# A two-layer graph-attention kernel: four-strip scores, smaller projection pieces, and a new order of work at the seams between batch entries

## The chip, the cores and the metric

The kernel runs on one core of one Trainium2 chip. The metric is the device time of one execution in microseconds (us); lower is better. Before the change three runs took 4387.88, 4392.93 and 4394.0 us, so the median is 4392.93 us. A separate profiled execution took 4391.85 us; its recorded span is 4389.8 us, and all durations below come from it.

Engines are called by the profile's names: PE is TensorE (PEld its weight loads), DVE is VectorE, ACT is ScalarE, POOL is GpSimd, SP is SyncE, which issues most of the DMAs.

## The reference

Input x has 8 batch entries of 2048 rows and 256 columns; adj is one 2048 x 2048 matrix of 0 and 1 for all entries. Two layers follow each other, each with a residual and a layer norm:

```python
# layer 0, for each entry: 8 heads of 32 columns
x_proj = einsum('bnd,hdf->bhnf', x, W)
e_src, e_dst = x_proj . a_src, x_proj . a_dst          # one number per row and head
e = leaky_relu(e_src[..., :, None] + e_dst[..., None, :], 0.2)
e = e + softplus(beta_tilde) * log(adj + 1e-6);  e = where(adj > 0, e, -huge)
h = softmax(e) @ x_proj;  x = layernorm(x + h.reshape(B, N, 256) @ W_out.T)
# layer 1, for each entry: one head of 256 columns
h1, h2, h3 = x @ W1, x @ W2, x @ W3
e = where(adj > 0, leaky_relu(h1 @ h2.T, 0.2), -huge)
x = layernorm(x + relu(softmax(e) @ h3))
```

All is in float32.

## The kernel before

**Layer 0 of an entry** is 64 steps (`Gat.step`, L320): 4 pairs of heads (`hp`) times 16 tiles of 128 source rows (`jt`). The exponential of the leaky score is split into factors of the two rows, so that a step needs no exponential: DVE makes, for each head of the pair, one 128 x 2048 tile `s` with one instruction (L336) from a row of factors `c` that is the same on all partitions, a column of factors `re` and the tile `mt` of the transposed mask. PE then adds `s` into the sums `val` (8 products) and mostly also into the denominators `den` (8 products), both in PSUM, in four strips of 32 output rows (`products`, L358). For some `jt`, listed in `SUMMED`, the `den` products are left out and DVE adds `s` into a tile `d` instead (L343; the first of them on ACT, L349). Four buffers hold `s`, two for each step, so DVE can be two steps ahead of PE. At the end of a head pair `finish` (L365) copies the sums to `ht` on ACT, takes the denominators through DRAM (`rc`, `rec_d`, `rb`) and, at every second pair, multiplies `ht` by their reciprocals on DVE (L389).

**The seam** leads an entry from layer 0 to layer 1. `output` (L391) yields four times; each time PE multiplies four row tiles of `ht` by W_out (products `y`, two row tiles in one PSUM buffer), DVE adds x and takes the statistics (L416 to L419), ACT normalises into `ht` (L425) and stores it. `turn` (L430) yields eight times; each time PE transposes two row tiles (`tr`, L439), ACT copies them to `x1t` (L440), and PE makes two row tiles of h3 (L445).

**Layer 1 of an entry** is 16 row tiles (`Dot`, L451). `scores` (L469) makes the 2048 scores `e` of a row tile on PE, adds the mask `pen` on DVE and takes the exponential on ACT into `p`, one row tile ahead; `Dot.step` (L484) transposes `p` (`pt`), and sums `acc` with h3.

**Interleaving.** The order of the PE instructions is the order of the program text; the framework orders the other engines. Layer 1 of entry b-1 is mixed with the layer 0 steps of entry b: `fill(0)`, `fill(1)` and `fill(2)` are the places in a `Dot.step` where steps (`layer_0`) or W_out products (`output`) are put. The last two row tiles of the entry before that are held back for the seam (L605, L606). All 64 steps of an entry are so spread over one period.

**Entry 0** has no layer 1 beside it. Its 64 steps are mixed with the projections of the other seven entries (`others`, L539): after every second step one group of four row tiles (`rows`, L255) with the eight transposes of x made one group ahead (`turn` in L549). There are 28 groups for 32 places. At an entry's last group `factors` (L268) and four `scale` (L282) run on DVE, and `store` (L288) sends v and re to DRAM; `queries` (L292) makes `c_d`. The entries come in the order 2, 3, 4, 5, 6, 7, 1; their `v` tiles take the two buffers "v" and "h3" in turn. Entry 1 stays in its buffer.

**The start.** `scores_first` (L246) makes the scores of entry 0 with the transposed x as the held operand and 16 moving columns: 32 products of 128 x 16.

PSUM has three buffers of 128 x 512 (`mm_tile`) that projections, transposes, y, e, tr and h3p share in turn. `chunk` has three buffers "ht" for `xg`, `xt`, `dn`, `h1` and adjacency rows.

## Time and profile before

| what | us |
|---|---|
| median of three runs | 4392.93 |
| span of the profiled execution | 4389.8 |
| PE idle, 0 to 100 | 23.5 |
| PE idle, 450 to 550 | 21.6 |
| PE idle, 1500 to 1600 | 6.8 |
| PE idle, 4000 to 4100 | 4.5 |
| granted PE clock, mean | 0.989 |

The table's idle times are the length of a stretch less PE's busy time in it. The page of a profile gives each engine's busy share, the share in 40 slices, the chain of work that ended last, and groups of instructions with count, busy time and mean duration. The order of time lists merged groups of one engine: start, length, engine, line, operation, output and inputs, and in brackets the idle time before it and what ended it. A matmul in float32 has two records. The lists of waits give total, number and longest.

### The profile page before, as it was taken

How to read it: one execution, taken by the hardware profiler on the slowest of the kernel's cores; microseconds unless marked ns; L12 is line 12 of the kernel's file. 1: busy time of each engine (PE TensorE's matmuls, PEld its weight loads, DVE VectorE, ACT ScalarE, POOL GpSimd, SP SyncE). 2: the span in 40 equal slices, each digit the busy share in tenths (PEclk: the TensorE clock that was granted, in tenths of full speed). 3: DMA queues.
4: the chain of work that ended last, by engine and by line, in shares of the span. 5: the costliest groups of instructions: out<-in, count | busy, mean ns of one | idle time of the engine just before them, and what ended most of it. 6: DMA issues, size and time to landing. Idle time of an engine off the chain costs nothing.

```text
span 4389.8 us, 59761 instructions
## 1 busy us (share of the span) xinstructions
PE 4243.0 (97%) x25052; PEld 2226.0 (51%) x25052; DVE 3624.5 (83%) x2597; ACT 1666.5 (38%) x3020; POOL 6.4 (0%) x14
## 2 busy tenths in 40 slices
PE   7899899999999999999999999999999999999999
PEld 5454344445444545445445454445555454545666
DVE  6888888998989898997989988898889889898222
ACT  6622233333333323333333334333333333333454
POOL 0000000000000000000000000000000000000000
PEclk9999999999999999999999999999999999999999
DMA  7887666656555554556555555556545565554111
GB/s 234 292 302 273 209 221 211 230 193 225 191 189 189 197 197 168 195 192 213 180 193 185 188 196 185 192 187 216 184 166 199 184 214 184 191 183 147 60 50 41
DMA packets 250958, 839.10 MB, mean 191 GB/s; under 512 B 32320, under 2 KB 150848, under 8 KB 175424
## 3 DMA queue, kind: packets, MB, share of 16 engines
q1 hardware_dynamic: 215360, 801.71, 52.1%
q10 hardware_dynamic: 35328, 33.56, 2.2%
q8 instruction: 196, 3.21, 0.3%
q14 instruction: 74, 0.61, 0.0%
HBM read 761.53 MB, written 73.14 MB: 190 GB/s over the span
## 4 chain that ended last, share of the span: by engine, by line
PE 56%; DVE 18%; issue 9%; DMA 4%; ACT 2%; SPq 1%; ACTq 0%; DVEq 0%
PE acc L510 15%; PE e L475 14%; DVE s L336 11%; PE val L361 11%; PE den L361 7%; DVE d L343 4%; PE pt L494 4%; DMA mt<-mt_d 3%; PE y L414 2%; PE h1p L465 2%; PE h3p L445 1%; DVE p L480 1%; ACT p L481 1%; DMA rc<-dn 1%; SPq L379 0%
## 5 line engine op out<-in xcount | busy, mean ns | idle before, releaser
L336 DVE SCALAR_TENSOR_TENSOR s<-c,re,mt 128x2048 f32<-128x2048 f32 x1024 | 2353.5, 2342 | 194.4 <-PE den L361 132.8
L361 PE MATMUL val<-s,v 128*32 128x512 f32 x8192 | 1030.0, 604 | 67.8 <-DVE s L336 67.3
L510 PE MATMUL acc<-h,pts 128*128 128x256 f32 x4096 | 949.9, 380 | 2.2 <-ACT pts L496 1.4
L475 PE MATMUL e<-x1t,h 128*128 128x512 f32 x2048 | 906.0, 595 | 6.8 <-ACT h L467 6.8
L510 PEld LDWEIGHTS acc<-h,pts 128*128 128x128 f32 x4096 | 748.1, 190 | 92.8 <-ACT pts L496 6.9
L361 PE MATMUL den<-s,re 128*32 128x512 f32 x5568 | 709.0, 599 | 3.3 <-ACT dn L376 3.3
L343 DVE SCALAR_TENSOR_TENSOR d<-s,re,d 128x2048 f32<-128x2048 f32 x272 | 632.2, 2344 | 0.0
L475 PEld LDWEIGHTS e<-x1t,h 128*128 128x128 f32 x2048 | 379.1, 190 | 459.5 <-issue 416.5
L496 ACT COPY pts<-pt 128x512 f32<-128x512 f32 x512 | 298.2, 583 | 766.4 <-PE pt L494 759.5
L361 PEld LDWEIGHTS val<-s,v 128*32 128x32 f32 x8192 | 244.3, 110 | 676.4 <-issue 516.3
L477 ACT ACTIVATE p<-e 128x512 f32<-128x512 f32 x512 | 303.1, 596 | 433.6 <-PE e L475 429.9
L480 DVE CUSTOM_DVE_ANT_0 p<-p,pen 128x2048 f32<-128x2048 f32 x128 | 292.9, 2288 | 198.2 <-ACT p L477 197.5
L361 PEld LDWEIGHTS den<-s,re 128*32 128x32 f32 x5568 | 194.3, 111 | 429.6 <-issue 417.0
L494 PEld LDWEIGHTS pt<-ident,p 128*128 128x128 f32 x2048 | 239.0, 141 | 223.2 <-issue 163.0
L481 ACT ACTIVATE p<-p,neg 128x2048 f32<-128x2048 f32 x128 | 256.7, 2006 | 242.4 <-DVE neg L480 242.4
L494 PE MATMUL pt<-ident,p 128*128 128x128 f32 x2048 | 319.3, 279 | 6.5 <-ACT p L481 6.5
L517 ACT ACTIVATE z<-acc,rec 128x256 f32<-128x256 f32 x128 | 60.9, 475 | 370.4 <-PE acc L510 340.0
L518 DVE TENSOR_TENSOR z<-z,x1r 128x256 f32<-128x256 f32 x128 | 53.8, 421 | 156.1 <-ACT z L517 155.9
L445 PE MATMUL h3p<-w3s,x1t 128*128 128x256 f32 x512 | 122.6, 383 | 15.4 <-ACT x1t L440 14.5
L414 PE MATMUL y<-wot,ht 128*128 128x256 f32 x512 | 120.5, 393 | 9.8 <-DVE ht L389 9.8
L262 PE MATMUL proj<-wp,xt 128*128 128x272 f32 (+1 forms) x512 | 125.5, 398 | 0.1
L349 ACT ACTIVATE d<-s,re 128x2048 f32<-128x2048 f32 x56 | 112.1, 2005 | 29.1 <-DMA mt<-mt_d 23.5
(85 smaller groups left out, 1877.3 us busy)
## 6 DMA issues: line engine op xcount, KB each, us to landing
mt<-mt_d SPq DMA_DIRECT2D x496, 1024.0 KB, 4.9
c<-c_d SPq DMA_DIRECT2D x64, 1024.0 KB, 7.1
pen<-pen_d SPq DMA_DIRECT2D x112, 512.0 KB, 3.4
xg<-in_x_dram SPq DMA_DIRECT2D x60, 512.0 KB, 6.0
adj_t<-in_adj_dram SPq DMA_DIRECT2D x16, 1024.0 KB, 7.9
mt_d<-mt SPq DMA_DIRECT2D x16, 1024.0 KB, 5.7
rb<-rec_d SPq DMA_DIRECT2D x64, 256.0 KB, 4.6
x_d<-ht ACTq DMA_DIRECT2D x32, 512.0 KB, 3.6
```

Of the source, the lines that this page charges most:

```text
L336: nc.vector.scalar_tensor_tensor(sa, self.cs[a], self.re[:, 0, jt, h:h + 1], mt, ALU.max, ALU.mult)
L343: nc.vector.scalar_tensor_tensor(d, sa, e[:, jt - 1, h:h + 1], d, ALU.mult, ALU.add)
L361: nc.tensor.matmul(dst[ts(q, DH), ts(c, BK)], weights[q % 2], s[q % 2][:, ds(q // 2 * HALF + c * BK, BK)], start=start, stop=stop)
L414: nc.tensor.matmul(y[:, i, :], self.ht[:, g * IG + k + i, kc, :], wot[:, kc, :], start=(kc == 0), stop=(kc == KC - 1))
L445: nc.tensor.matmul(t[:, ts(i, D)], x1t[:, kc, ts(2 * (j - 1) + i, P)], w3s[:, kc, :], start=(kc == 0), stop=(kc == KC - 1))
L475: nc.tensor.matmul(t, self.h1[:, kc, ts(it % IG, P)], self.x1t[:, kc, ts(c, BK)], start=(kc == 0), stop=(kc == KC - 1))
L477: nc.scalar.activation(p[:, ts(c, BK)], t, AF.Prelu, alpha=ALPHA)
L480: nc.vector.tensor_tensor_reduce(p, p, pen, -1.0, FMAX, ALU.add, ALU.min, neg)
L481: nc.scalar.activation(p, p, AF.Exp, bias=neg, scale=-1.0, accum_out=den)
L494: nc.tensor.transpose(t[:, ts(k, P)], p[:, ts(g * IG + k, P)], ident)
L496: nc.scalar.copy(pt, t)
L510: nc.tensor.matmul(acc, now[:, ts(k, P)], self.h3[:, j, :], start=(j == 0), stop=(j == NT - 1))
```

## The change

1. `scores_first` holds the weight columns (padded with zeros to 32, so `wp` is 16 columns wider) and moves the transposed x, in four strips: 8 products of 32 x 512. The result is copied to SBUF, transposed back by four transposes, and copied into `both`.
2. `others` yields after each row tile instead of each group of four (`rows` becomes `row`). The loop over entry 0's steps takes, after every second step, so many row tiles that the 112 are spread evenly over the 32 places: 3 and 4 in turn. The weights' preparation comes at each second step past 16 until it is done.
3. The entries come in the order 2, 3, 4, 5, 1, 6, 7. The buffers are still taken in turn, but entry 7, the last, takes "h3", as entry 6 does, since entry 1 stays in "v". `re` has three buffers.
4. Seams: the second held row tile has no W_out products in it; behind it come two times "two groups of W_out products, two steps". In `turn` two steps follow every second yield up to the sixth instead of one after each. At entry 0's seam four steps, the products in two halves and two steps.
5. `output` loads x two groups ahead.

```diff
+            t = mm_tile("scores")
+            for kc in range(KC):
+                for q in range(NB):
+                    nc.tensor.matmul(t[ts(q, DH), :], wp[:, kc, D:], xt[:, kc, ts(q, BK)],
                                      start=(kc == 0), stop=(kc == KC - 1))
+            s = chunk.tile([P, BK], F32, tag="pt", name="scores", bufs=2)
+            nc.scalar.copy(s, t)
+            t = mm_tile("scores_t")
+            for k in range(IG):
+                nc.tensor.transpose(t[:, ts(k, P)], s[:, ts(k, P)], ident)
...
-        items = [(gat, g) for gat in gats[2:] + gats[1:2] for g in range(NB)]
+        order = gats[2:-2] + gats[1:2] + gats[-2:]
...
-                gat.begin(("v", "h3")[n // NB % 2])
+                gat.begin("h3" if n // NB % 2 or gat is order[-1] else "v")
...
-        if k % 2 == 1:
-            next(pieces[0], None)
-            if k > NT and k % 4 == 1:
-                next(pieces[1], None)
+        if k % 2 == 0:
+            for _ in range(k * count // (NP * NT) - (k - 2) * count // (NP * NT)):
+                next(projections)
+            if k > NT:
+                next(weights, None)
...
-            layer_0(3)
-            output(4)
-            layer_0(1)
+            layer_0(4)
+            output(2)
+            next(projections)
+            output(2)
+            layer_0(2)
         else:
             dot.step(lambda k: layer_0((0, 0, 2)[k]))
-            dot.step(lambda k: (output((1, 1, 2)[k]), layer_0((0, 1, 1)[k])))
-        for _ in gat.turn():
-            layer_0(1)
+            dot.step()
+            for _ in range(2):
+                output(2)
+                layer_0(2)
+        for k, _ in enumerate(gat.turn()):
+            if k % 2 == 1 and k < 7:
+                layer_0(2)
         dot = Dot(gat)
-        dot.step(lambda k: layer_0((2, 1, 1)[k]))
+        dot.step(lambda k: layer_0((2, 0, 2)[k]))
```

More of the change, by code (lines that the diff above doesn't have):

```diff
@@ L105 @@
     beta_c = beta[:, 3:4]
-    wp = const.tile([P, KC, D + 2 * H], F32)
+    wp = const.tile([P, KC, D + DH], F32)
+    nc.vector.memset(wp[:, :, D + 2 * H:], 0.0)
     for kc in range(KC):
@@ L113 @@
         )
-    for a, dst in ((a_dst, wp[:, :, D:D + H]), (a_src, wp[:, :, D + H:])):
+    for a, dst in ((a_dst, wp[:, :, D:D + H]), (a_src, wp[:, :, D + H:D + 2 * H])):
         a_bc = small.tile([P, D], F32, tag="row", name="a_bc", bufs=4)
@@ L246, in scores_first, with row @@
         def scores_first(self, xt):
-            t = mm_tile("both")
-            for it in range(NT):
-                for kc in range(KC):
-                    nc.tensor.matmul(t[:, ts(it, 2 * H)], xt[:, kc, ts(it, P)], wp[:, kc, D:],
+            t = mm_tile("scores")
+            for kc in range(KC):
+                for q in range(NB):
+                    nc.tensor.matmul(t[ts(q, DH), :], wp[:, kc, D:], xt[:, kc, ts(q, BK)],
                                      start=(kc == 0), stop=(kc == KC - 1))
-            nc.scalar.copy(self.both.rearrange("p t h -> p (t h)"), t[:, 0:NT * 2 * H])
-        def rows(self, g, xt, scores=True):
-            cols = D + 2 * H if scores else D
-            for k in range(IG):
-                it = g * IG + k
-                t = mm_tile("proj")
-                for kc in range(KC):
-                    nc.tensor.matmul(t[:, 0:cols], xt[:, kc, ts(k, P)], wp[:, kc, 0:cols],
-                                     start=(kc == 0), stop=(kc == KC - 1))
-                nc.scalar.copy(self.v[:, it, :], t[:, 0:D])
-                if scores:
-                    nc.scalar.copy(self.both[:, it, :], t[:, D:cols])
+            s = chunk.tile([P, BK], F32, tag="pt", name="scores", bufs=2)
[3 more added lines that the diff above has]
+                nc.tensor.transpose(t[:, ts(k, P)], s[:, ts(k, P)], ident)
+            nc.scalar.copy(self.both.rearrange("p (q k) h -> p k q h", k=IG),
+                           t.rearrange("p (k q h) -> p k q h", k=IG, h=DH)[:, :, :, 0:2 * H])
+        def row(self, it, xt, scores=True):
+            cols = D + 2 * H if scores else D
+            t = mm_tile("proj")
+            for kc in range(KC):
+                nc.tensor.matmul(t[:, 0:cols], xt[:, kc, ts(it % IG, P)], wp[:, kc, 0:cols],
+                                 start=(kc == 0), stop=(kc == KC - 1))
+            nc.scalar.copy(self.v[:, it, :], t[:, 0:D])
+            if scores:
+                nc.scalar.copy(self.both[:, it, :], t[:, D:cols])
         def factors(self):
@@ L277, in factors @@
             nc.vector.tensor_tensor(ed, ed, top[:, 1:2, :].to_broadcast([P, NT, H]), ALU.subtract)
-            self.re = small.tile([P, 2, NT, H], F32, name="re", bufs=2)
+            self.re = small.tile([P, 2, NT, H], F32, name="re", bufs=3)
             nc.scalar.activation(self.re[:, 0], ed, AF.Exp, scale=-(1.0 - ALPHA))
@@ L302, in load @@
             nc.sync.dma_start(self.v, v_d[self.b])
-            self.re = small.tile([P, 2, NT, H], F32, name="re", bufs=2)
+            self.re = small.tile([P, 2, NT, H], F32, name="re", bufs=3)
             nc.sync.dma_start(self.re, re_d[self.b])
@@ L400, in load @@
                 nc.sync.dma_start(xs[g], xb[:, ts(g, IG), :])
-            for g in range(NB - 1):
-                load(g)
+            load(0)
+            load(1)
             for g in range(NB):
-                if g == 1:
-                    load(NB - 1)
+                if g + 2 < NB:
+                    load(g + 2)
                 st = small.tile([P, IG, nc.vector.BN_STATS_DIM], F32, name="st4", bufs=1)
@@ L531 @@
     for g in range(NB):
-        g0.rows(g, xt0[:, :, ts(g, BK)], False)
+        for k in range(IG):
+            g0.row(g * IG + k, xt0[:, :, ts(g, BK)], False)
         g0.scale(g)
@@ L539, in others @@
     def others():
-        items = [(gat, g) for gat in gats[2:] + gats[1:2] for g in range(NB)]
+        order = gats[2:-2] + gats[1:2] + gats[-2:]
+        groups = [(gat, g) for gat in order for g in range(NB)]
         xgs, xts = [], []
         def load(n):
-            if n < len(items):
-                xgs.append(load_x(items[n][0].b, items[n][1]))
+            if n < len(groups):
+                xgs.append(load_x(groups[n][0].b, groups[n][1]))
         def turn(n):
-            if n < len(items):
+            if n < len(groups):
                 xts.append(chunk.tile([P, KC, BK], F32, tag="ht", name="xt", bufs=3))
@@ L556, in others @@
         turn(0)
-        for n, (gat, g) in enumerate(items):
+        for n, (gat, g) in enumerate(groups):
             turn(n + 1)
             if g == 0:
-                gat.begin(("v", "h3")[n // NB % 2])
-            gat.rows(g, xts[n])
-            if g == 0 and n > 0:
-                items[n - 1][0].queries()
-            if g == NB - 1:
-                gat.factors()
-                for k in range(NB):
-                    gat.scale(k)
-                if gat.b > 1:
-                    gat.store()
-            yield
-        gats[1].queries()
+                gat.begin("h3" if n // NB % 2 or gat is order[-1] else "v")
+            for k in range(IG):
+                gat.row(g * IG + k, xts[n])
+                if g == NB - 1 and k == IG - 1:
+                    gat.factors()
+                    for i in range(NB):
+                        gat.scale(i)
+                    if gat.b > 1:
+                        gat.store()
+                if g == 0 and k == IG - 1 and n > 0:
+                    groups[n - 1][0].queries()
+                yield
+        order[-1].queries()
         yield
-    pieces = [others(), later_weights()]
-    for k in range(NP * NT):
+    projections, weights = others(), later_weights()
+    count = (B - 1) * NT
+    for k in range(1, NP * NT + 1):
         g0.step()
-        if k % 2 == 1:
-            next(pieces[0], None)
-            if k > NT and k % 4 == 1:
-                next(pieces[1], None)
+        if k % 2 == 0:
[3 more added lines that the diff above has]
+                next(weights, None)
     dot = None
```

## The prediction

> **What bounds the kernel now.** First the page's busy shares, then the waits of TensorE, then the order of time at three places.

> ```profile
> PE 4243.0 (97%) x25052; PEld 2226.0 (51%) x25052; DVE 3624.5 (83%) x2597; ACT 1666.5 (38%) x3020; POOL 6.4 (0%) x14
> ...
> PE val L361 <- DVE s L336: 67.3, 46, 5.7
> PE h3p L445 <- ACT x1t L440: 14.5, 8, 2.7
> ...
> PE y L414 <- DVE ht L389: 9.8, 2, 6.3
> ```

> PE is busy 97%, so at most 147 us can be won without removing products; 67.3 of them wait for the VectorE tiles `s`. The idle times come in three places. The start (0 to 160 us) holds 32 us of them. The steps 57 to 64 of entry 0 and its seam, from the order of time:

> ```profile
> 458.64 1.04 PE L361 MATMUL val<-s,v 128*32 128x512 f32 x2 [3.61 <-DVE s L336]
> 460.90 2.78 PE L361 MATMUL val<-s,v 128*32 128x512 f32 x11 [1.22 <-DVE s L336]
> ...
> 516.73 3.78 PE L414 MATMUL y<-wot,ht 128*128 128x256 f32 x8 [6.29 <-DVE ht L389]
> ```

> Here no projection is left, a step costs VectorE 2 x 2.27 = 4.53 us and PE 3.6, so PE waits at each step. And the later seams, the same to 0.1 us in each period of 509 us:

> ```profile
> 1536.16 1.04 PE L361 MATMUL val<-s,v 128*32 128x512 f32 x2 [1.53 <-DVE s L336]
> 1539.80 2.78 PE L361 MATMUL val<-s,v 128*32 128x512 f32 x11 [2.60 <-DVE s L336]
> ...
> 1567.01 1.99 PE L445 MATMUL h3p<-w3s,x1t 128*128 128x256 f32 x8 [2.70 <-ACT x1t L440]
> ...
> 1602.19 1.04 PE L361 MATMUL val<-s,v 128*32 128x512 f32 x2 [0.84 <-DVE s L336]
> 1604.45 1.49 PE L361 MATMUL val<-s,v 128*32 128x512 f32 x11 [1.22 <-DVE s L336]
> ```

> That is 8.9 us of idle a seam. Eleven records of `val` take 2.78 us at 1539.80 and 1.49 at 1604.45: the first ran at half clock, which costs 2.7 us more. VectorE itself stands idle there 1523.4 to 1529.05 (5.60, for y), 1554.2 to 1556.3 (2.11) and 1567.9 to 1572.6 (4.54).

> [...]

> **The change, part by part.**

> Scores in strips. `both` (L251) holds PE from 15.72 to 25.74, 10.0 us for 64 records, mostly at half clock. The new form: 8 products in four strips at `val`'s 1.8 us (3.3 at half clock, row at 61.10), a 128x512 copy 0.59, four transposes 0.66, latencies 0.3. PE gets to the projections near 19.0, 6.7 us earlier. Not all behind it follows. In the built order VectorE makes the second `m` (L180) ahead of `top`, and its `adj_t` comes with the first loads, which keep the DMA engines busy to 23.5; so `top` starts near 24.8 instead of 26.34. The second `c` load now stands on SP's queue behind the first `mt_d` store. Against that, `m` (L183) comes before the factors' scaling and is done near 28.4 instead of 36.2, which removes the 4.09 us wait at 56.41. DMA is at 0.97 from 100 to 150 us and can take some back. Gain between 2 and 10; I take 7. The memset of `wp` is VectorE work under the weights' load (idle 3.98 to 8.13): nothing.

> Projections in pieces of 3 or 4 rows at all 32 second steps (before: 4 rows at 28). PE's work is the same. The 8 steps without it are filled: their PE idle is 3.61+1.22+1.22+4x0.89+0.42 = 10.0, half clock some 3 more. Three things give it back.
> (a) Entry 7 now projects into "h3" directly behind entry 6 in the same buffer. In ScalarE's built order the first `v` copy of entry 7 waits for the store of entry 6's `v`, and behind it stand all later copies out of PSUM. The store can start after `top`, one `s` (2.27), the factors (about 2) and four scalings (4.63): about 9.7 us after the last row of entry 6; it lands 8.2 us later (median of the six v_d stores), so near 18. PE has two transposes, two rows, a pair of steps (7.2) and a third row until it needs the blocked PSUM buffer: 11. It stalls 7, with clock 8. Below: 0, if the store overtakes; above: 12.
> (b) The last factors fall behind step 64. With den of step 64 as zero: VectorE makes `s` 0 and 1 of entry 1 to 5.6, waits for `rc` to 7.5, then top, factors, scalings to 15, `s` 2 to 19.6, `s` 3, two `d` adds and `ht` to 31. PE: 4 rows (3.8), steps 0 and 1 to 9.2, stands to 19.6, step 2 to 22.7, step 3 from 28.8 to 30.6, then y. Before, y began at 27.0 (489.74 to 516.73) without step 3 (1.8).
> (c) The denser steps meet the scaling bursts: 0.5 us at each of five, 2.5.
> Step 64 ends at 489.7-3.8-13+8+2.5 = 483.4, y begins at 514.0, worth 512.2 against 516.7: 4.5 gained. After y VectorE has eight y tiles and `s` 4, 5 to make before step 5, to 53.8, where before it had 50.5; PE loses 3.5 there. Gain 1, between -6 and 16.

> Seams of entries 1 to 6 (six). I walk VectorE in the built order from 1523.4, with the trace's durations. `s` 2a, 2b, 3a when buffers free (1525.4) to 1532.2; idle until row 15's z, 1536.9, as acc now stands before y (PE: 4 transposes and 4 acc groups, 8.9, to 1536.2). y 0 to 3 with `s` 3b among them (8 adds, 16 statistics pairs cost 1.5 a tile as at 521 to 535) to 1548.1; `s` 4 to 1552.6; y 4 to 7 and two `d` adds to 1563.1; `s` 5 to 1567.7. Before: 1568.0, so equal. PE stands from 1559.2 (den of step 4) to 1567.7, one long wait in place of 1.53, 2.60 and 2.70. From there VectorE runs on, where before it waited 4.54 for step 4: `s` 6 to 13 (16x2.26) and six `d` adds to 1621.8; then p, exp, pt at 1626.4. PE has its e at 1620.5 and steps 12, 13 to 1626. Before: 1627.9. Gain 1.5 a seam, 9 in all; from -3 to +5 each. xg is now asked for one group at a time: two are loaded ahead, and the fourth load waited for the first group's add before too; hidden. The moved steps' loads on SP: `mt` of step 3 stood behind that fourth load (1531.49, 1531.90) and now goes ahead of it; `mt` of step 5 now stands behind it, so behind the first group's adds (near 1542), and lands about 5 us after that, 15 before `s` 5a at 1563; `pen`, `c` and `re` keep their places between. Hidden too. The output's normalisation on ScalarE (2.08 a group against 3.5 of PE) is hidden by the y products.

> Last seam (entry 7, no steps beside it): y waited 3.56 for `ht` at 4068.79; now pt and acc of row 15 (8.9) lie in front. Gain 3.5 (1 to 4).

> Sum: 7+1+9+3.5 = 20.5; I take off 1.5 for semaphore times that a walk leaves out: 19. Against its own span 4389.8 that is 4371; the timed runs lie at 4387.9 to 4394.0 with median 4392.9, so 4374.

> **The rivals.**
> 1. The waits go as the shape suggests: VectorE's free time before y is filled and PE doesn't stand at step 5. For: 12.3 us of VectorE idle a seam. Against: the built order puts y's statistics and `d` ahead of `s` 5. It would give 7 a seam, 18 at entry 0's end, 7 and 3.5: 70, 4323.
> 2. Nothing to measure: DMA takes the start back (2), entry 0's end and the seams come out at zero, 3.5 at the last: 4387.
> 3. Slower: VectorE is the bound of the new seam. Place: from the first y add to `s` 5b, 29.5 us in my walk, and the chain behind it without slack. If a y tile costs 1.73 (as at 1529.05 to 1530.77, alone) instead of 1.5 and PE at half clock after its 8.5 us wait frees the `s` buffers 3.5 later, the seam loses 4 instead of gaining 1.5; it decides from 31 us on. 6x4 = 24, entry 0's end -6, the start 2, the last 3.5: 4417.
> 4. That the change doesn't do what it says is excluded: the built order shows each move.

> **How the numbers follow.** Forecast 0.45, own range 4362 to 4386; rival 1 0.20; rival 2 0.18; rival 3 0.17. A measurement tells about 0.2% (8.8 us: 4384.1 to 4401.7) from no change. Faster: rival 1 and nearly all of the forecast, 0.63; same 0.19; slower 0.18. The range takes in rival 2, most of rival 1 and the lower edge of rival 3: 4328 to 4400.

> **What would show it.** `proj` begins near 19 us. One wait of about 8 us of `val` for `s` at step 5 in each seam, no more 2.70 of `h3p` for `x1t`. A PE wait on ScalarE's `v` copy, some 45 us ahead of step 64's end, behind a v_d store. No 3.56 at the last y. The forecast is wrong if the 509 us period shortens or lengthens by over 3 us, or if PE has no two waits between step 64 and y.

## The result, and the profile after

The changed kernel takes 4369.7 us (median of four, 4367.7 to 4370.3) against 4391.3 for the kernel before beside it: ratio 0.995, interval 0.9933 to 0.9968. A second measurement (below) gave 0.9952, 0.9939 to 0.9966. The profiled execution spans 4368.3 us, 21.5 less than that of before.

First the busy shares on the page of the changed kernel, then its TensorE's waits (engine, tile and line, what it waits for: us in total, times, longest).

```profile
PE 4226.0 (97%) x25008; PEld 2221.4 (51%) x25008; DVE 3618.2 (83%) x2598; ACT 1669.7 (38%) x3021; POOL 9.5 (0%) x14
```
```profile
PE val L367 <- DVE s L342: 69.2, 37, 6.0
PE h3p L451 <- ACT x1t L446: 2.6, 9, 0.7
```

The `h3p` wait is gone, as forecast (14.5 to 2.6), but `val` waits for `s` as long as before: fewer waits (37 for 46) of greater length. The waits listed do not show the gain. It is found by cutting both traces at instructions that both have, once in each period. "xg" is the first transpose of the second x group (the line that waits for the load), "e" the `e` product that waits for `h1` in mid-period, "h1p" the first `h1p` behind a seam.

| stretch | before | after | gain | forecast |
|---|---|---|---|---|
| start to xg | 71.27 | 63.23 | 8.0 | 7 |
| xg to the first h1p (entry 0, first seam) | 510.00 | 512.98 | -3.0 | 1 |
| seam behind entry 1 (e to h1p) | 186.96 | 189.44 | -2.5 | 1.5 |
| five seams after it, together | 925.90 | 913.84 | 12.1 | 7.5 |
| last seam (e to h1p) | 144.00 | 137.88 | 6.1 | 3.5 |
| all between the seams, and the end | 2551.67 | 2550.93 | 0.7 | 0 |

The gains sum to 21.4 against 20.5 before the forecast's 1.5 for semaphores. The total was nearly right; of the parts that were to gain something only the start was right to 1 us.

Now the lines that answer to those of before, from the order of time. The start and the end of entry 0:

```profile
18.89 0.66 PE L259 MATMUL scores_t<-ident,scores 128*128 128x128 f32 x4 [0.68 <-ACT scores L256]
63.23 1.94 PE L173 MATMUL tr<-ident,xg 128*128 128x128 f32 x8 [6.52 <-DMA xg<-in_x_dram]
...
446.00 2.18 PE L268 MATMUL proj<-wp,xt 128*128 128x272 f32 x4 [6.49 <-ACT both L272]
494.39 1.91 PE L367 MATMUL val<-s,v 128*32 128x512 f32 x2 [6.01 <-DVE s L342]
505.76 2.46 PE L367 MATMUL val<-s,v 128*32 128x512 f32 x14 [3.75 <-DVE s L342]
508.16 8.27 PE L420 MATMUL y<-wot,ht 128*128 128x256 f32 x32
```

The scores are in by 19.5 and the transposes come 8 us earlier, though their own load wait grew from 4.12 to 6.52. The store wait is there (6.49; that it is the store is shown by a run below), and so are two waits between step 64 and y (6.01, 3.75), as forecast.

The seam that stood at 1536 to 1604, PE and then VectorE:

```profile
1561.64 1.92 PE L367 MATMUL val<-s,v 128*32 128x512 f32 x2 [5.41 <-DVE s L342]
1563.97 2.04 PE L367 MATMUL val<-s,v 128*32 128x512 f32 x11 [0.41 <-DVE s L342]
...
1600.24 1.92 PE L367 MATMUL val<-s,v 128*32 128x512 f32 x14 [0.88 <-DVE s L342]
```
```profile
1524.23 6.88 DVE L342 SCALAR_TENSOR_TENSOR s<-c,re,mt 128x2048 f32<-128x2048 f32 x3 [3.88 <-DMA mt<-mt_d]
1533.91 0.42 DVE L524 TENSOR_TENSOR z<-z,x1r 128x256 f32<-128x256 f32 x1 [2.80 <-ACT z L523]
...
1538.58 0.69 DVE L422 TENSOR_TENSOR ht<-y,xg 128x512 f32<-128x512 f32 x1 [0.95 <-PE y L420]
```

TensorE has one long wait, at step 5. After 1538.58 VectorE shows no wait until behind the next `p`. The busy time by stretch says the same. The columns are the stretch, its length, then busy us of PE, PEld, DVE, ACT and POOL with the number of records, TensorE's clock, the DMA share and GB/s. Of before, and of the changed kernel, from the s of step 5 to h1p and then the whole seam from e to h1p:

```profile
1567.90:1611.79 43.89, 41.84 (x294) 19.83 (x293) 39.35 (x20) 10.17 (x18) 0.00 (x0) 1.00 0.48 169
1426.36:1611.79 185.43, 176.55 (x1066) 95.18 (x1067) 160.59 (x133) 63.22 (x118) 0.00 (x0) 0.98 0.55 196
```
```profile
1563.90:1606.04 42.14, 40.44 (x270) 21.51 (x271) 42.14 (x21) 10.49 (x19) 0.00 (x0) 0.99 0.53 187
1423.28:1606.04 182.76, 175.01 (x1066) 95.90 (x1067) 162.68 (x134) 62.88 (x117) 0.00 (x0) 0.98 0.58 201
```

Before, VectorE stood 43.89 - 39.35 = 4.54 us there (its wait for step 4); now it is busy for 42.14 of 42.14. Over the whole seam VectorE's idle time fell from 24.8 to 20.1 us, while it did 2.1 us more work; the difference is the 2.7 us by which this seam is shorter. That it is VectorE's time that counts, and not TensorE's, is tested below.

The last seam, before and after:

```profile
4068.79 6.14 PE L414 MATMUL y<-wot,ht 128*128 128x256 f32 x14 [3.56 <-DVE ht L389]
```
```profile
4058.11 13.98 PE L420 MATMUL y<-wot,ht 128*128 128x256 f32 x64
```

The wait of 3.56 is gone. Fourteen y records took 6.14 us behind it, with a recorded clock of 0.50 (4067.77 to 4074.59); at the rate of the later line (13.98 for 64, clock 1.00) they take 3.1. So half clock had cost about another 3.

### The profile page after: what moved, and what is told of

Same layout as the page of the kernel before. It is cut to its first block, busy times and chain, and to the rows that moved or that the text cites. A ratio compares the mean times of both kernels' runs of the same rounds, so it can differ in the third digit from the quotient of the medians.

```text
span 4368.3 us, 59747 instructions
## 1 busy us (share of the span) xinstructions
PE 4226.0 (97%) x25008; PEld 2221.4 (51%) x25008; DVE 3618.2 (83%) x2598; ACT 1669.7 (38%) x3021; POOL 9.5 (0%) x14
## 4 chain that ended last, share of the span: by engine, by line
PE 64%; DVE 16%; issue 7%; DMA 2%; ACT 2%; SPq 0%; ACTq 0%; DVEq 0%; POOLq 0%
PE acc L516 18%; PE e L481 16%; PE val L367 13%; DVE s L342 10%; PE den L367 9%; PE pt L500 5%; DVE d L349 4%; DMA mt<-mt_d 2%; PE h1p L471 1%; PE y L420 1%; PE proj L268 1%; DVE st L424 1%; DVE ht L422 1%; PE h3p L451 1%; DVE p L486 0%
## 5 line engine op out<-in xcount | busy, mean ns | idle before, releaser
L524 DVE TENSOR_TENSOR z<-z,x1r 128x256 f32<-128x256 f32 x128 | 53.8, 421 | 178.7 <-ACT z L523 175.3
L268 PEld LDWEIGHTS proj<-wp,xt 128*128 128x128 f32 x512 | 93.3, 192 | 51.4 <-issue 21.0
```

The lines of the kernel that those rows point to most:

```text
L268: nc.tensor.matmul(t[:, 0:cols], xt[:, kc, ts(it % IG, P)], wp[:, kc, 0:cols], start=(kc == 0), stop=(kc == KC - 1))
```

## The experiments

Theory: at the start TensorE's own chain sets the time; in the seams VectorE's total work does, not the order in it and not TensorE's long wait. Rivals stand with each run. Ratios are to the kernel before, run beside; intervals of 95%. The table of stretches, which is finer than the times, uses the profile of each run.

**Each part alone on the kernel before.** The start alone:

```diff
-    wp = const.tile([P, KC, D + 2 * H], F32)
+    wp = const.tile([P, KC, D + DH], F32)
...
+                    nc.tensor.matmul(t[ts(q, DH), :], wp[:, kc, D:], xt[:, kc, ts(q, BK)],
```

> The kernel before with the scores in four strips alone (and the padded weights they need). Theory (the start is bound by TensorE's chain from the transposes to the projections, and nothing later gives it back): projections begin near 19.4 us as in the changed kernel, the transposes of the second x group and every later fixed point come 8 us earlier, the span falls by 8 us (4382). Rival (the DMA engines, busy at 0.97 from 100 to 150 us, set the end of this stage): projections begin near 19.4 all the same, but the gain shrinks to under 3 us by 160 us and the span falls by 0 to 3.

Measured: 4385.5 us, ratio 0.9987 (0.998 to 0.9993): 5.7 off. The projections begin at 20.9 us, not 19.4, and xg is at 64.07, that is 7.2 earlier than in the profile of before; 511.46 from there to the first h1p, against 510.0. The theory holds in the main, with 1 to 2 us given back: 8 were expected. The start varies by itself: the three kernels with the old scores have xg at 68.94 to 71.65 (mean 70.6), the eleven with strips at 63.23 to 66.64 (mean 64.8). So 5.9 is the better figure, and the 8.0 of the first table is partly this variation.

Entry 0's pieces, its order and its seam alone:

```diff
-        items = [(gat, g) for gat in gats[2:] + gats[1:2] for g in range(NB)]
+        order = gats[2:-2] + gats[1:2] + gats[-2:]
...
-            layer_0(3)
-            output(4)
-            layer_0(1)
+            layer_0(4)
+            output(2)
+            next(projections)
+            output(2)
+            layer_0(2)
```

> The kernel before with entry 0's pieces of 3 or 4 row tiles, its order of entries and its seam (the first) alone. Theory (the filled steps give about 13, the store wait takes about 8, the factors behind step 64 take most of the rest): step 64 ends 4 to 7 us earlier than before, y begins 2 to 3 earlier, and after that seam 3 to 5 are lost again, so the end of the first seam (the first h1p behind it) comes 0 to 3 us later than before, and the span is within 3 us of 4390. Rival (the pieces are worth more and the changed kernel's start is what gave something back): the first seam ends over 4 us earlier than before and the span falls by over 4.

Measured: 4398.2 us, ratio 1.0014 (1.0008 to 1.0021): 6.1 longer. xg to the first h1p takes 515.85. The expected band of 3 us was too small and the rival has the wrong sign: alone, this part costs. Over all kernels with these pieces and this order of entries (the changed kernel twice, this one, and three below that share the code so far) the stretch is 510.9 to 515.9, mean 513.5; with the old pieces 510.0 to 511.5, mean 510.7. The cost is 2.7 in these profiles. This run's own times give more, 3.5 to 9.2 by its interval, so alone this part may cost more than beside the others; that was not tried further.

The seams of entries 1 to 7 alone:

```diff
-            dot.step(lambda k: (output((1, 1, 2)[k]), layer_0((0, 1, 1)[k])))
+            dot.step()
+            for _ in range(2):
+                output(2)
+                layer_0(2)
```

> The kernel before with the seams of entries 1 to 7 alone. Theory (each seam's time is set by VectorE's chain from the first y add to the s of step 5, whatever came before entry 1): the period of 508.6 us falls to 506.1 for five entries, the seam behind entry 1 loses 2.0, the last gains 5.8: 12.7 - 2.0 + 5.8 = 16.5 off the span, 4373. Rival (part of the seams' gain comes from the state that entry 0's new end leaves): period above 507 and under 12 us off the span.

Measured: 4374.8 us, ratio 0.9959 (0.9947 to 0.9972): 18 off. Seams of 182.8 (before 184.4 to 185.8, mean of three kernels 185.3), the last 137.89, the one behind entry 1 188.51. The seams came out as expected, so they don't depend on how entry 0 ended; the periods, 506.0 to 507.2 where 506.1 was expected, differ by what lies between the seams. This run holds the held row tile, the steps in `turn` and the loads of x together; which of them gives how much was not tried. The three parts sum to -5.7 + 6.1 - 18 = -17.6, against -21 to -22 for all together, within the intervals.

**The seam behind entry 1, which loses.** There `pt` of row 15 waits 4.37 us for exp of `p`, because VectorE makes this row's mask first; in the kernel before a group of y products stood in that gap. Its TensorE in the changed kernel, then TensorE and VectorE in the kernel before:

```profile
1017.35 1.97 PE L500 MATMUL pt<-ident,p 128*128 128x128 f32 x8 [4.37 <-ACT p L487]
1055.29 1.04 PE L367 MATMUL val<-s,v 128*32 128x512 f32 x2 [3.63 <-DVE s L342]
```
```profile
1032.57 1.91 PE L361 MATMUL val<-s,v 128*32 128x512 f32 x2 [5.39 <-DVE s L336]
1030.16 2.35 DVE L336 SCALAR_TENSOR_TENSOR s<-c,re,mt 128x2048 f32<-128x2048 f32 x1 [1.25 <-DMA mt<-mt_d]
```

One kernel puts the y products back, in this seam alone:

```diff
+            held = dot.b == 0
+            if held:
+                output(1)
             dot.step()
-            for _ in range(2):
-                output(2)
+            for k in range(2):
+                output(2 - (held and k == 0))
                 layer_0(2)
```

> The changed kernel, with one group of y products put back ahead of the transposes of row 15 in the seam behind entry 1 alone (this seam's p waits for a mask that VectorE makes, so exp of p ends only at 1017.3 us while PE is free from 1012.9). Theory (these y products hid the wait for p in the kernel before, and their move cost this seam its loss): the wait of 4.37 us of pt for p goes to under 1, its transposes and acc products run at full clock, and the span falls by 3 to 5 us against the changed kernel. Rival (the s of step 5, which VectorE's chain fixes, sets this seam): the 4.37 goes, the 3.63 wait at step 5 grows by as much, and the span moves by under 1.

Measured: 4374.7 us, ratio 0.9959 (0.9945 to 0.9972), no better than the changed kernel; the seam takes 189.24, against 188.5 to 189.8 without the edit. TensorE's and VectorE's lines there:

```profile
1017.32 1.09 PE L500 MATMUL pt<-ident,p 128*128 128x128 f32 x8 [1.23 <-ACT p L487]
1034.40 1.04 PE L367 MATMUL val<-s,v 128*32 128x512 f32 x2 [0.67 <-DVE s L342]
1037.38 1.92 PE L367 MATMUL val<-s,v 128*32 128x512 f32 x14 [1.93 <-DVE s L342]
1054.85 1.91 PE L367 MATMUL val<-s,v 128*32 128x512 f32 x2 [4.88 <-DVE s L342]
```
```profile
1024.76 4.62 DVE L342 SCALAR_TENSOR_TENSOR s<-c,re,mt 128x2048 f32<-128x2048 f32 x2 [5.17 <-DMA mt<-mt_d]
```

The wait for `p` went from 4.37 to 1.23 and came back as waits for `s`. The rival was right that the seam doesn't move; but more came back ahead of step 5 (0.67 and 1.93) than at it (4.88 for 3.63). So the wait for `p` is not what this seam loses by. VectorE stands 5.17 for the `mt` of step 2, where the kernel before stood 1.25 at this place. What sets this load's time, and whether an earlier one would save the seam, was not tried; the cause of this loss stays open.

**What sets the later seams.** Two edits to VectorE's sums in the first pair of heads of entries 2 to 7, the pair that runs in the seams. One only moves work behind the s of step 5:

```diff
-                chain = SUMMED[self.b]
+                chain = (1, 4, 6, 8, 11, 13) if self.b > 1 and hp == 0 else SUMMED[self.b]
```

> The changed kernel; in the first pair of heads of entries 2 to 7 VectorE sums step 4 instead of step 3 into its d tiles, so the two d adds (2 x 2.27 us) stand behind the s of step 5 instead of ahead of them, and VectorE's work in all is the same. Theory (VectorE's total work from the first y add to the p of the next row sets a seam, the order in it does not): the wait of 5.41 us at step 5 goes to under 1.5, later waits for s take its place, and the span moves by under 4 us against the changed kernel. Rival (the long wait at step 5 itself, with the half clock behind it, is what a seam costs): 4 to 7 us less in each of five or six seams, 20 to 40 off the span.

Measured: 4374.8 us, ratio 0.9962 (0.9949 to 0.9976). The 5.41 at step 5 became 2.43 (under 1.5 was expected), four later waits (0.34, 1.22, 0.34, 1.22) stand where two (0.41, 0.50) stood, and the seam takes 182.89 against 182.77. The rival, 20 to 40 off, is out: the long wait is a symptom. So is the half clock behind it: the first two of these seams have a recorded clock of 1.00, where the changed kernel's has 0.98, and are as long.

The other takes two d adds out (five sums instead of six) and puts one `den` on TensorE:

```diff
-                chain = SUMMED[self.b]
+                chain = (1, 4, 8, 11, 13) if self.b > 1 and hp == 0 else SUMMED[self.b]
```

> The changed kernel; in the first pair of heads of entries 2 to 7 five steps are summed on VectorE instead of six (1, 4, 8, 11, 13): two d adds less (4.53 us of VectorE), one den of eight products more (1.72 us of TensorE). Theory (VectorE's total work sets the seam): each seam that such a pair stands in becomes 2.5 to 4.5 us shorter, the period 506.1 falls to 502 to 503.5, and the span by 12 to 25. Rival (TensorE sets it, VectorE's waits only fill what would be idle anyway): 1.7 longer in each, the span up to 10 longer.

Measured: 4356.2 us, ratio 0.992 (0.9906 to 0.9933), some 13 below the changed kernel. The run before it is its control: that one moves step 3 to 4 too, so leaving out step 6 is all that differs. A seam of it (its five take 179.0 to 180.5), and one with four sums (below), both from e to h1p:

```profile
1927.90:2107.24 179.34, 175.48 (x1083) 96.04 (x1083) 158.52 (x132) 62.89 (x117) 0.00 (x0) 0.99 0.58 205
```
```profile
1915.22:2092.84 177.62, 175.49 (x1098) 96.81 (x1099) 154.07 (x130) 62.88 (x117) 0.00 (x0) 1.00 0.60 207
```

VectorE lost 4.2 us of work and the seam 3.4, with more products on TensorE. That is the theory, within its 2.5 to 4.5, for these five seams. The seam behind entry 1 has two d adds less as well, and takes 189.61 against 190.25 in the control: there the theory gives too much.

**The end of entry 0.** The order of entries, so that no entry is projected into a buffer whose store has still to run:

```diff
-        order = gats[2:-2] + gats[1:2] + gats[-2:]
+        order = gats[2:-1] + gats[1:2] + gats[-1:]
...
-                gat.begin("h3" if n // NB % 2 or gat is order[-1] else "v")
+                gat.begin(("h3", "v")[n // NB % 2])
```

> The changed kernel with the entries projected in the order 2, 3, 4, 5, 6, 1, 7 and the buffers h3 and v in turn, so that no projection goes into a buffer directly behind an entry whose store is still to run. Theory (the wait of 6.49 us of the third row of entry 7 is the store of entry 6's v, and TensorE has VectorE's s tiles ahead at that place): the wait goes, nothing takes its place, and y begins 5 to 8 us earlier; the span falls by as much. Rival (VectorE is the bound of these steps, the store wait only lies where PE would wait for s): other waits take its place, and y begins within 2 us of where it did.

Measured: 4365.9 us, ratio 0.9943 (0.9931 to 0.9956). In its order of time the store wait has become:

```profile
450.87 1.49 PE L367 MATMUL val<-s,v 128*32 128x512 f32 x11 [0.89 <-DVE s L342]
492.28 1.91 PE L367 MATMUL val<-s,v 128*32 128x512 f32 x2 [6.93 <-DVE s L342]
```

From xg to y it takes 442.1 us, and 439.6 and 440.1 in the two kernels below with the same order; with the store wait 443.7 to 448.8 in six profiles. The mean moves from 446.2 to 440.6: 5.6 us, inside the expected 5 to 8. To the first h1p the same: 513.5 to 507.7. The wait was real, and little took its place. The timed gain is smaller: by the ratios 3 to 4 us under the changed kernel, where 5 to 8 were expected; the intervals don't decide between the two.

The last factors ahead of step 64 instead of behind it:

```diff
-            for _ in range(k * count // (NP * NT) - (k - 2) * count // (NP * NT)):
+            upto = [min(count, i * count // 60) for i in (k - 2, k)]
+            for _ in range(upto[1] - upto[0]):
```

> The changed kernel with the 112 row tiles of entries 1 to 7 spread over the first 60 steps of entry 0 instead of 64, so that the last factors and scalings (6.6 us of VectorE) stand ahead of step 64. Theory (the factors behind step 64 are what makes TensorE wait 6.01 and 3.75 us in steps 1 to 3 of entry 1, since VectorE is idle for 6.33 + 2.60 + 0.81 us just before): both waits go to under 2, the two or three unfilled steps cost about 1 us each, and y begins 4 to 8 us earlier from the same start. Rival (VectorE's total work to the first y sets the place): the waits move ahead of step 64, and y begins within 2 us of where it did.

Measured: 4381.3 us, ratio 0.9974 (0.9963 to 0.9984), some 10 slower than the changed kernel. From xg to the first h1p 520.45. Its VectorE:

```profile
493.54 0.35 DVE L386 RECIPROCAL rc<-rc 128x32 f32<-128x32 f32 x1 [1.61 <-DMA rc<-dn]
497.68 4.61 DVE L342 SCALAR_TENSOR_TENSOR s<-c,re,mt 128x2048 f32<-128x2048 f32 x2 [1.61 <-DMA mt<-mt_d]
505.05 4.74 DVE L342 SCALAR_TENSOR_TENSOR s<-c,re,mt 128x2048 f32<-128x2048 f32 x2 [2.75 <-DMA mt<-mt_d]
```

The rival was right up to y, which comes 446.8 us after xg (mean of the changed order 446.2). But 6.4 more are lost behind y's first record, which neither said; 1.92 of it is a wait of the y products themselves, for the scaling of `ht`. With the factors gone from behind step 64, VectorE stands for the loads of `rc` and `mt` there (5.97 us in these lines), where in the changed kernel it has no such wait between step 64 and y. The factors had filled the time of these loads. Behind y TensorE waits 4.30 for `s`, against 1.70 and 1.35; why that grew so much is open. This kernel also leaves the last steps of entry 0 without row tiles, and the two effects were not separated.

**The changed kernel again, and what the findings add up to.**

> The changed kernel once more, as the measure of the three that run beside it. Theory: its start, entry 0 and first seam take a time that varies by 2 to 3 us from one execution to the next (loads), while its period stays at 506.1 us and the seam behind entry 1 at about 2 us over that of the kernel before; the ratio to the kernel before lies between 0.994 and 0.997. Rival: the period varies as well, by over 0.5 us, and what was read from single profiles says little.

Measured: 4374.6 us, ratio 0.9952 (0.9939 to 0.9966). Seams of 182.77 again but for one of 183.07, the one behind entry 1 189.82; xg at 65.53, entry 0 514.62. The period is steady, the start and entry 0 vary, as the theory has it.

The order and five sums together (the two edits above):

```diff
-        order = gats[2:-2] + gats[1:2] + gats[-2:]
+        order = gats[2:-1] + gats[1:2] + gats[-1:]
...
-                chain = SUMMED[self.b]
+                chain = (1, 4, 8, 11, 13) if self.b > 1 and hp == 0 else SUMMED[self.b]
```

> The changed kernel with two edits together: the order 2, 3, 4, 5, 6, 1, 7 of the projections, and five summed steps (1, 4, 8, 11, 13) instead of six in the first pair of heads of entries 2 to 7. Theory (the two act at different places and add): 13 off for the sums and 3 to 5 for the order, so 4352 and 16 to 18 under the changed kernel beside it. Rival (the order's gain is given back at the seams): within 3 us of the sums alone, 13 off.

Measured: 4345.7 us, ratio 0.9895 (0.9882 to 0.9909): 25 under the changed kernel beside it by the ratios, more than the 16 to 18 expected, though each ratio is known to some 6 us only; the seam behind entry 1 fell too, to 186.68, which neither edit did alone (189.61 and 188.77); with four sums it is 184.09 (next run), with five again 187.47 (the last).

The same with four sums:

```diff
-                chain = (1, 4, 8, 11, 13) if self.b > 1 and hp == 0 else SUMMED[self.b]
+                chain = (1, 8, 11, 13) if self.b > 1 and hp == 0 else SUMMED[self.b]
```

> As the kernel of the order and five sums, with four summed steps (1, 8, 11, 13) in the first pair of heads of entries 2 to 7. Theory (with five sums the waits for s that are left in a seam, 1.03 + 1.22 and 0.64 of pt, are nearly as long as the one den of 1.72 us that a further sum off VectorE puts on TensorE, so the bound passes from VectorE to TensorE here): the period moves by -1.5 to +0.5 us and the span by -8 to +3 against five sums. Rival (VectorE still sets the whole seam): 2.5 less in each of six, 15 off. Rival (TensorE set it already): 1.7 more in each, 10 longer.

Measured: 4335.8 us, ratio 0.9871 (0.9857 to 0.9884), the fastest kernel of the study. Each of the five seams takes 177.6 (one 177.95) instead of 179.1, the edge of what was expected; the timed gain, 0.0024 or 10.5 us, lies outside the -8 to +3. The size was missed, the turn was not: two d adds off VectorE bought 3.4 to 3.8 us of a seam the first time and 1.5 the second, and TensorE is now busy for 175.5 of 177.6.

The same idea in the first seam, on the kernel of the order and five sums:

```diff
-                chain = (1, 4, 8, 11, 13) if self.b > 1 and hp == 0 else SUMMED[self.b]
+                chain = SUMMED[self.b]
+                if self.b > 0 and hp == 0:
+                    chain = (1, 4, 8, 12) if self.b == 1 else (1, 4, 8, 11, 13)
```

> As the kernel of the order and five sums, with the first pair of heads of entry 1 summed in four steps (1, 4, 8, 12) instead of five (1, 3, 6, 9, 12), so that the first seam too has two d adds less. Theory (VectorE sets the first seam as well, from the last factors to the h1p): the first h1p comes 1.5 to 4.5 us earlier from the same start, and the span falls by as much against five sums. Rival (the first seam is set by the loads of mt and by TensorE): within 1 us or up to 1.7 later.

Measured: 4345.5 us, ratio 0.9894 (0.988 to 0.9907), no gain seen; xg to the first h1p 505.93, without the edit 506.06. But without the edit this stretch is also 508.8 and 508.1 (the kernels of the order alone and of four sums), so a gain of 1 or 2 us can't be excluded. The 4.5 us of VectorE's work that two d adds take did not come off the first seam: the theory of the later seams isn't shown to carry over to this one.

## Why the prediction was right, point by point

- **The total** was forecast at 4374 and measured at 4369.7; it is faster, as the likeliest case said. But the rows erred in both directions: entry 0 and the seam behind entry 1 by 8 us to the bad, the five seams and the last by 7.2 to the good. So the nearness of the total is in part luck.
- **Start, 7:** right. 5.9 over fourteen profiles, 8.0 in the one pair. The projections begin at 19.39 (forecast near 19.0), 6.4 earlier, and the wait of 4.09 at 56.41 is gone; 2.4 went back into the wait for x, 6.5 in place of 4.1.
- **Entry 0, store wait (a), 7, with clock 8:** right in cause and size. It measured 6.49 (6.5 to 7.4 in seven profiles), and taking its cause away gave 5.6. That ScalarE's later copies stand behind the one that waits was the author's assumption; in the trace the `v` copy waits 11.39 us for `v_d` and starts at 445.50, and the five copies after it start at 445.77 to 446.42. The recorded clock is 0.50 from 442.15 to 448.98. The wait stands 33 us ahead of step 64's end, not 45.
- **Entry 0, last factors (b):** the walk's times were good (y 29.0 us behind step 64's end, forecast 30.6, and both waits where they were said to be). The reading was wrong: the step counted the factors as a loss. In the run with the factors ahead of step 64 VectorE stands for the loads of `rc` and `mt` in their place, and y comes no earlier; that run is also slower, by an amount that is explained in part only.
- **Entry 0's sum, +1:** measured -2.7, inside its -6 to 16. In the one pair (-3.0), counted from xg, step 64 ends 2.5 us earlier than before where the walk has 6.3, so 3.8 are missing ahead of it; 1.6 come back up to y, and behind y 5.3 are lost where the walk has 3.5. The changed kernel also shows four waits of `proj` for ScalarE's `xt` and `both` copies, 1.12, 1.12, 0.98 and 0.98, in the steps where the masks are made (84 to 138 us), which the kernel before doesn't list. The forecast looked only at the end of entry 0. That these 4.2 us are the missing 3.8 is argued from the trace, not tried; the 1.8 behind y stay open.
- **Seams, 1.5 each:** the mechanism was right (VectorE runs on behind step 5 where it stood 4.54; one long wait at step 5) and the size off: 2.6 each over three kernels of before. The chain from the first y add, put at 29.5 us, took 28.7 (1535.13 to 1563.84), so this term was 0.8 too dear. The wait came out at 5.41, not 8.5, since TensorE goes on with the first of the two s and waits again for the second.
- **The seam behind entry 1 taken as one of six equals, 1.5:** this step failed. It loses 2.7 over eight profiles, 2.5 in the one pair. The working used 1523 us as the model of all six, as "the same to 0.1 us". They were not the same: before the change this seam took 186.96 against 184.4 to 185.5, and had a wait of 5.39 where the model has 1.53 and 2.60; it is the one in which VectorE makes masks. Rival 3, a seam that gets longer because VectorE is its bound, is shown for it in part only: two d adds less gave 0.6 here, 1.3 to 2.1 with the order changed too, against 3.4 in the later seams. Why the change made it longer stays open.
- **Last seam, 3.5:** mis-sized. The idle time fell by 3.4 as said (5.0 to 1.6), but the half clock behind a wait of 3.56 us was left out of this one term, and was worth 2.7: 6.1 in all.
- **Rival 1 (70 us less)** fell on what the forecast held against it: VectorE's order puts y's statistics and d ahead of s 5. But the run that put two d adds behind s 5 gained nothing either; it is the work, not the order.
- **The clock.** What the prediction adds for half clock (1 in (a), some 3 for the eight steps, 3.5 in rival 3) was the author's estimate. Its own line at 1539.80 has half clock behind a wait of 2.60 (recorded clock 0.50 from 1538.50 to 1545.33); the last section has what the traces show.

## What to carry to other kernels

When two engines are both near their limit in a stage, ask how much work each has between two fixed points, not which wait is longest: the 5.41 us wait could be moved and split, and the stage stayed 182.8 us; taking 4.2 us of work off VectorE cut it by 3.4. Before taking one seam as the model of all, look at the odd one, where something else (here the masks) is made as well. And an operation that stands on the critical path may be filling the time of a load, as the last factors did here (5.97 us of waits for loads in their place): what it hides must be named before it is moved.

## What was not expected of the hardware

```profile
527.48:530.89 3.41, 1.42 (x6) 0.14 (x2) 3.41 (x4) 1.22 (x3) 0.00 (x0) 1.00 0.56 190
530.89:534.30 3.41, 2.35 (x12) 0.59 (x16) 3.41 (x4) 1.25 (x4) 0.00 (x0) 0.50 0.41 79
```
```profile
529.08:532.49 3.41, 2.00 (x20) 0.39 (x12) 3.41 (x8) 1.06 (x4) 0.00 (x0) 1.00 0.59 187
532.49:535.90 3.41, 1.75 (x10) 0.42 (x14) 3.41 (x5) 2.47 (x6) 0.00 (x0) 1.00 0.07 25
```

In the first, TensorE is busy for 1.42 of a step's 3.41 us, and the next step runs at half clock. In the second the waits are shared by two steps, busy for 2.00 and 1.75, and the clock stays. Counted over the steps of the profile of before and the first of the changed kernel (70 to 4340 us), every full-clock step with TensorE busy (as the profile records it) for under 0.41 of it was followed by half clock (27 of 27), none with 0.49 or more (0 of 2422), and 1 of the 4 between. So half clock went with how much of one step the waits took up, and the length of a single wait did not decide: the same 1.7 and 1.35 us came before both.

A part worth 2 or 3 us can't be priced from one profile. Not all of that is the clock: the stretches between seams (the first left out) take 323.1 to 325.3 us, with three of 326.1 to 327.2. In each of these three `acc` waits 1.8 to 2.3 us for `pts`, and in two of them the recorded clock is 1.00 throughout. The longest has this line, which the stretches beside it don't have:

```profile
3295.98 1.99 PE L516 MATMUL acc<-h,pts 128*128 128x256 f32 x8 [2.30 <-ACT pts L502]
```
